# Linear's first three blocks turned by transfers and VectorE from stored rows, the third one's input in the first one's place

## The chip, the cores and the metric

The kernel runs on one core of a Trainium2 chip. The metric is the device time of one execution in microseconds, and the time of the kernel is the median of several runs. A core has TensorE (PE, with its weight loads shown as PEld), VectorE (DVE), ScalarE (ACT), GpSimd (POOL) and SyncE (SP, which here only issues transfers), each with an instruction stream of its own that runs in order.

## What is computed

Two layers over 2 x 1024 tokens of 512 numbers, four sub-layers in all, each followed by a residual sum and a layernorm. The change lies in the second sub-layer, called Linear here, and touches the end of the first one and the start of the third.

```python
x = _layernorm(x + _L0_attn_ref(x, ...))          # state-space layer
x = _layernorm(x + _L0_ffn_ref(x, weight, scale)) # Linear: the place of the change
x = _layernorm(x + _L1_attn_ref(x, ...))          # recurrence: branches, gates, scans
x = _layernorm(x + _L1_ffn_ref(x, ...))           # gated feed-forward

def _L0_ffn_ref(x, weight, scale):                # weight is 512 x 512, of -1, 0 and 1
    out = jnp.einsum('bln,nk->blk', x, weight) * scale
    v_norm = jnp.maximum(jnp.linalg.norm(out, axis=-1, keepdims=True), EPS)
    out = out * (jnp.tanh(v_norm) / (v_norm + EPS))
    o_norm = jnp.maximum(jnp.linalg.norm(out, axis=-1, keepdims=True), EPS)
    return out * jnp.minimum(0.99 / o_norm, 1.0)
```

## The kernel before

The tokens are worked on in four blocks of 512 (`NBLK`), block b in four groups of 128 rows (`NJ`). A block's rows lie in a tile `X[b]` of 128 partitions x 4 x 512. For a product with TensorE the block is needed turned, with its 512 columns on the partitions in four pieces of 128 (`NK`). There are two ways to turn one in this kernel.

`transposed` (L226) does it on TensorE: per piece k four 128x128 transposes (L237) into a PSUM bank, from which ScalarE or VectorE copies. With `split`, ScalarE casts the bank to fp32r (L241), and VectorE subtracts the cast from the bank (L244): two fp32r pieces, `wu0` and `wd0`, stand for one fp32 operand, and each product is made of two matmuls.

The other way has two halves. `load_blocks` (L261) loads the block's rows from DRAM in four DMAs of 256 KB, which set runs of 32 numbers (128 bytes) where the 32x32 squares of the turned block belong. `turn_blocks` (L271) then turns the 32x32 squares within each piece with four VectorE instructions (L273). It needs the rows in DRAM, where `conclude` stores them (`x_mid`, L791, and L799 for block 0).

Linear's block b is the generator `linear(b)` (L968). It makes the two pieces, yields, makes four row groups of products `po` (L987, eight matmuls each) with a scaling on VectorE (L991) and a sum of squares on ScalarE (L993), yielding after two and after four. Then come the chain of small operations for the norms (L997 to L1009), the residual sum (L1011), and `layernorm` with its last step (L291) on POOL, all but one row group of block 0, which is VectorE's. From block 1 on the rows are stored as `x_lin`. Blocks 0, 1 and 2 are turned by `transposed`, the last block by `load_blocks` into `mid` (L1063), `turn_blocks` and `split` (L951), which casts from SBUF (L955) and subtracts (L957).

`conclude` (L762) ends the first layer for a block: per row group j eight matmuls `po` (L770) with a yield in the middle, and VectorE's row sum into `X` (L785). Between the row groups of the last block, `weave` (L304) puts steps of `linear(0)` and `linear(1)`: plan entry i says how many steps follow step i of `conclude`. Then `weave` joins `linear(2)` with the first block's `branches(0)` of the recurrence, which turns X[0] with `transposed` into tile `w4` and makes products with w_x and w_y (`p`, L1069, in `product`). `gates(0)` (L1109) makes products of the convolved `cv`, with `linear(3)` between them.

The program's text sets a priority only: a scheduler orders each engine's instructions, and an instruction under `keep_in_program_order` stays behind everything that stands before it in the text on its engine. Tiles of one tag share a place in a pool, and a pool lays out its tags in the order in which they first appear. The pools `ep` and `wp` lie where the first layer's tiles were; what is loaded there waits for the last reader of what lay there. w_f0 (L900) waits for the scan products' end, X[0] and X[1] (L903) for the last reader of `w_in`, w_x (L909) for POOL's `sums` (L759). Tag `lo` of `ep` is first used by `coming_block` (L962), tag `w4` of `wp` by `branches(0)`; the places of `w0` to `w3` come first. SP issues all these loads from one queue: w_f0, X[0], X[1], the scale row f0s, w_x, w_y, X[2], twelve small parameter loads (`parameters`, L856, whose `softplus` of a_param gives VectorE a dozen small operations), then w_ig, w_ag (L1029) and the first integer weights `st` (L927).

The layers are written out a second time (`later_layers(False)`), behind a test of the weights that is false with these inputs.

Of the kernel before, what the change touches and what calls it, by code (L numbers as in the profile page):

```python
# [9 lines left out]
F32 = mybir.dt.float32  # L10
# [3 lines left out]
ALU = mybir.AluOpType  # L14
PSUM = bass.MemoryType.PSUM

P = 128
TB = 512
NJ = TB // P
D = 512  # L20
NK = D // P
# [16 lines left out]
def model_kernel(ctx: ExitStack, tc: tile.TileContext, t: dict, out: bass.AP):  # L38
    nc = tc.nc
    ctx.enter_context(nc.allow_non_contiguous_dma(reason="small parameter columns"))  # L40
    BATCH, SEQ, _ = t["L0_attn_hidden_states"].shape
    NBLK = BATCH * SEQ // TB
# [3 lines left out]
    x_mid = tc.dram_tile([NBLK, TB, D], F32, name="x_mid")  # L46
# [35 lines left out]
    X = [tokens() for _ in range(3)]  # L82
# [140 lines left out]
        nc.vector.tensor_scalar(r, z, 0.0, None, ALU.max)  # L223
        nc.vector.scalar_tensor_tensor(o, p, 2.0, r, ALU.mult, ALU.add)

    def transposed(pool, b, X, tags=("xT",), split=False, bufs=1, by_act=False, behind=False, soon=False):  # L226


        pieces = [
            pool.tile([P, NK, TB], F32R if split else F32, tag=tag, name=f"{tag}{b}", bufs=bufs)  # L230
            for tag in tags
        ]
        xT = pieces[0]
        for k in range(NK):
            pt = bank("pt")
            for j in range(NJ):
                nc.tensor.transpose(  # L237
                    pt[:, j * P : (j + 1) * P], X[b][:, j, k * P : (k + 1) * P], ident
                )
            if split:  # L240
                copied = nc.scalar.copy(xT[:, k, :], pt)  # L241
                if behind:
                    tc.keep_in_program_order(copied)
                nc.vector.tensor_tensor(  # L244
                    pieces[1][:, k, :], pt, xT[:, k, :].bitcast(F32), ALU.subtract
                )
            elif soon:
                with tc.high_priority():
                    nc.scalar.copy(xT[:, k, :], pt)
            elif k % 2 or by_act:  # L250
                nc.scalar.copy(xT[:, k, :], pt)
            else:
                nc.vector.tensor_copy(xT[:, k, :], pt)
        return pieces
# [6 lines left out]
    def load_blocks(dst, rows, pinned=False):  # L261

        blocks = rows.rearrange("(n t) (k a c) -> a t k n c", t=32, k=NK, c=32)
        for a in range(4):
            load = nc.sync.dma_start(
                dst[32 * a : 32 * a + 32].rearrange("t k (n c) -> t k n c", c=32), blocks[a]
            )
            if pinned:
                tc.keep_in_program_order(load)

    def turn_blocks(dst, src=None, pinned=False):  # L271
        for k in range(NK):
            turned = nc.vector.transpose(dst[:, k, :], (src or dst)[:, k, :])  # L273
            if pinned:
                tc.keep_in_program_order(turned)
# [28 lines left out]
    def weave(main, fill, plan, rest=True):  # L304

        for i, _ in enumerate(main):
            for _ in range(plan[i] if i < len(plan) else 0):
                next(fill, None)
        for _ in fill if rest else ():
            pass  # L310
# [451 lines left out]
    def conclude(b, st):  # L762


        xc, sums = st["xc"], st["sums"]
        rms = sp.tile([P, NJ], F32, tag="rms", name="rms")
        for j in range(NJ):
            po = bank("po")
            for m in range(NX):
                nc.tensor.matmul(  # L770
                    po, xc[:, m, j * P : (j + 1) * P], w_out[:, m, :],
                    start=(m == 0), stop=(m == NX - 1),
                )
                if m == NX // 2 - 1:
                    yield
            if j == 0:
                pss = bank("pss")
                for i in range(NJ):
                    nc.tensor.matmul(
                        pss[:, i : i + 1], sums[:, i * P : (i + 1) * P], ones,  # L780
                        start=True, stop=True,
                    )
                nc.scalar.activation(rms, pss[:, :NJ], AF.Sqrt, bias=eps, scale=1.0 / DI)
                nc.vector.reciprocal(rms, rms)
            nc.vector.scalar_tensor_tensor(  # L785
                X[b][:, j, :], po, rms[:, j : j + 1], X[b][:, j, :], ALU.mult, ALU.add
            )
            yield
        if b:
            layernorm(X[b], pinned=b == NBLK - 1)  # L790
            store_rows(x_mid[b], X[b])  # L791
# [15 lines left out]
    H, before, st = None, None, {}  # L807
# [10 lines left out]
    for b in range(NBLK):  # L818
# [22 lines left out]
        before, st = st, coming  # L841
# [43 lines left out]
    def later_layers(exact, last=None):  # L885
# [4 lines left out]
        X = Y  # L890
# [8 lines left out]
        w_f0 = ep.tile([P, NK, D], F32, tag="wF", name="w_f0" + suffix)  # L899
        nc.sync.dma_start(w_f0, w_f0_source)  # L900
        rows_mid = [x_mid[b].rearrange("(j p) d -> p j d", p=P) for b in range(NBLK)]
        for b in range(2):
            nc.sync.dma_start(X[b], rows_mid[b])  # L903
        w1 = [
            wp.tile([P, NK, D], F32, tag=f"w{i}", name=f"w1{i}{suffix}") for i in range(4)
        ]
# [41 lines left out]
            wf = ep.tile([P, NK, D], F32, tag="wg0", name="wfg")  # L948
            nc.vector.tensor_copy(wf, w_f0)

        def split(x, pieces):  # L951


            for k in range(NK):
                nc.scalar.copy(pieces[0][:, k, :], x[:, k, :])  # L955
                if exact:
                    nc.vector.tensor_tensor(  # L957
                        pieces[1][:, k, :], x[:, k, :], pieces[0][:, k, :].bitcast(F32),
                        ALU.subtract,
                    )  # L960
# [7 lines left out]
        def linear(b):  # L968

            tags = ("wu0", "wd0") if exact else ("wu0",)  # L970
            if b == NBLK - 1:
                turn_blocks(mid)
                w1.append(wp.tile([P, NK, D], F32, tag="w4", name="w14" + suffix))
                xT = [ep.tile([P, NK, TB], WT, tag=tag, name=f"{tag}{b}") for tag in tags]
                split(mid, xT)
                nc.sync.dma_start(w1[4], w_sources["w_out"])
            else:

                xT = transposed(ep, b, X, tags=tags, split=exact, behind=b == 2)
            yield  # L980
            o = ep.tile([P, NJ, D], F32, tag="wF", name="o" + suffix)
            ssq = sp.tile([P, NJ], F32, tag="ssq", name="ssq")
            for j in range(NJ):
                po = bank("po")
                for k in range(NK):
                    for x in xT:
                        nc.tensor.matmul(  # L987
                            po, x[:, k, j * P : (j + 1) * P], wf[:, k, :],
                            start=(k == 0 and x is xT[0]), stop=(k == NK - 1 and x is xT[-1]),
                        )  # L990
                nc.vector.tensor_tensor(o[:, j, :], po, f0s, ALU.mult)  # L991
                junk = ep.tile([P, GW], mybir.dt.bfloat16, tag="junk", name="junk2")
                nc.scalar.activation(junk, o[:, j, :], AF.Square, accum_out=ssq[:, j : j + 1])  # L993
                if j % 2:
                    yield
            norm = sp.tile([P, NJ], F32, tag="norm", name="norm")
            nc.scalar.activation(norm, ssq, AF.Sqrt)  # L997
            v = sp.tile([P, NJ], F32, tag="v", name="v")
            nc.vector.tensor_scalar(v, norm, 1e-7, None, ALU.max)
            f = sp.tile([P, NJ], F32, tag="f", name="f")  # L1000
            nc.scalar.activation(f, v, AF.Tanh)
            nc.vector.tensor_scalar(v, v, 1e-7, None, ALU.add)
            nc.vector.reciprocal(v, v)
            nc.vector.tensor_tensor(f, f, v, ALU.mult)
            nc.vector.tensor_tensor(norm, norm, f, ALU.mult)
            nc.vector.tensor_scalar(norm, norm, 1e-7, None, ALU.max)
            nc.vector.reciprocal(norm, norm)
            nc.vector.tensor_scalar(norm, norm, 0.99, 1.0, ALU.mult, ALU.min)
            nc.vector.tensor_tensor(f, f, norm, ALU.mult)  # L1009
            for j in range(NJ):  # L1010
                nc.vector.scalar_tensor_tensor(  # L1011
                    X[b][:, j, :], o[:, j, :], f[:, j : j + 1], X[b][:, j, :],
                    ALU.mult, ALU.add,
                )
            layernorm(X[b], engine=nc.gpsimd, last=None if b else nc.vector)
            if b:
                store_rows(x_lin[b], X[b])
            yield

        if last:  # L1020
            steps, free = last

            weave(steps, itertools.chain(linear(0), linear(1)), (0, 1, 0, 2, 0, 1, 0, 2, 1))
            free()
        else:
            for _ in itertools.chain(linear(0), linear(1)):
                pass
        for i, name in ((2, "w_ig"), (3, "w_ag")):
            nc.sync.dma_start(w1[i], w_sources[name])  # L1029
# [28 lines left out]
        with tc.tile_pool(name="rec" + suffix, bufs=1, side="right", reuse_waits="tile") as rp:  # L1058
# [125 lines left out]
                yield  # L1184

            st = {}
            weave(branches(0, st), linear(2), (1,) * 4)
            lin = [coming_block(1)]
            bout = row("L1_attn_b_out", D, c1, nc.sync, "scale")
            ys = []  # L1190
# [254 lines left out]
```

## Time and profile before

| what | value |
|---|---|
| median of 3 runs | 1117.68 us (1117.55 to 1117.88) |
| profiled execution | 1116.89 us, span 1115.1 us, mean granted TensorE clock 0.998 |
| TensorE transposes at L237 | 96 in all, 0.273 us each; 64 of them from 416.4 to 458.7 us |
| VectorE transposes at L273 | 40 in all, 0.66 to 0.71 us each |
| `conclude` of the last block | po from 408.8 to 446.3 us |
| `linear(0)`, `(1)`, `(2)`, `(3)` products | from 424.7, 447.8, 461.9 and 500.1 us |
| VectorE busy, 410 to 420, 420 to 430, 430 to 440, 440 to 450 us | 9.26, 3.75, 6.24, 8.87 us |

Times in the text are microseconds from the start of the span. A line such as `416.58 1.81 PE pt L237 x16` in the chain of waits reads: from 416.58 on, for 1.81 us, the chain ran through 16 TensorE instructions of line 237, which write tile `pt`. In a line of the busy times by window stand the window, its length, then busy time and number of instructions for PE, PEld, DVE, ACT and POOL, the granted TensorE clock, the share of the DMA engines that was busy, and GB/s. In a row of one source line stand minimum, median and maximum in ns, then the first and last start in us.

### The profile page before, as it was taken

The page shows a single profiled execution, that of the slowest core. Times are in us where ns is not written, and L with a number is a line of the kernel's source. Part 1 is how long each engine was busy: PE and PEld are TensorE (multiplying, and loading weights), DVE is VectorE, ACT ScalarE, POOL GpSimd, SP SyncE. Part 2 cuts the span into 40 slices and gives each one's busy share as a digit, 9 for nine tenths or more (in the row PEclk, how much of TensorE's full clock was granted, in tenths as well). Part 3 has the DMA queues.
Part 4 walks back from the last instruction along what each step waited for, and adds up shares of the span by engine and source line. Part 5 has one row for each costly group of instructions (what it writes and reads, how often), then busy time and mean ns, then how long its engine had stood idle before and what let it go on. Part 6 is the DMA issues. An engine that isn't in the chain of part 4 may idle for free.

```text
span 1115.1 us, 12073 instructions
## 1 busy us (share of the span) xinstructions
PE 1099.4 (99%) x4450; PEld 663.3 (59%) x4450; DVE 701.4 (63%) x1267; ACT 451.4 (40%) x690; POOL 366.8 (33%) x347
## 2 busy tenths in 40 slices
PE   8999999999999999999999999999999999999996
PEld 5455445445544555745444444447888888888885
DVE  5989797797869676875727437184238866325224
ACT  3334624463454233556653372553223224224223
POOL 1547471565348240254433231236511001001000
PEclk9999999999999999999999999999999999999999
DMA  8005200911210137245650001304544002100001
GB/s 323 21 9 126 91 1 17 253 30 39 105 81 0 39 135 215 57 94 123 113 113 37 1 1 49 27 0 143 189 94 76 1 1 63 14 1 30 8 1 41
DMA packets 122059, 77.04 MB, mean 69 GB/s; under 512 B 94512, under 2 KB 95312, under 8 KB 120456
## 3 DMA queue, kind: packets, MB, share of 16 engines
q1 hardware_dynamic: 120792, 75.77, 25.7%
q8 instruction: 37, 0.61, 0.2%
q10 hardware_dynamic: 976, 0.39, 0.1%
q14 instruction: 30, 0.25, 0.1%
q0 software_dynamic: 224, 0.02, 0.0%
HBM read 59.95 MB, written 16.02 MB: 68 GB/s over the span
## 4 chain that ended last, share of the span: by engine, by line
PE 80%; DVE 11%; ACT 4%; issue 2%; POOL 2%; DMA 1%; SPq 0%; DVEq 0%; ACTq 0%; POOLq 0%
PE pgu L1039 20%; PE p L1069 16%; PE po L1270 10%; PE pg L372 9%; PE px L372 7%; PE po L770 6%; DVE acc L298 3%; PE po L1159 2%; PE py L705 2%; DVE L L578 2%; PE po L987 2%; PE pxt L674 1%; PE pt L237 1%; POOL x L1165 1%; PE py L697 1%
## 5 line engine op out<-in xcount | busy, mean ns | idle before, releaser
L1050 DVE SCALAR_TENSOR_TENSOR h<-pgu,L_ffn_up_scale,sg 128x512 f32<-128x512 f32 x63 | 47.1, 748 | 126.4 <-PE pgu L1039 122.6
L372 PE MATMUL px<-xT,w_in 128*128 128x512 f32 x256 | 114.6, 597 | 0.0
L593 POOL TENSOR_TENSOR L<-L,gm 128x512 f32<-128x512 f32 x64 | 93.5, 1490 | 63.7 <-DVE bdec L588 34.7
L372 PE MATMUL pg<-xT,w_in 128*128 128x512 f32 x256 | 113.5, 594 | 0.0
L770 PE MATMUL po<-w_out,xc 128*128 128x512 f32 x256 | 112.5, 593 | 0.7 <-DVE L L578 0.7
L1069 PE MATMUL p<-cv,w 128*128 128x512 f32 x256 | 110.8, 592 | 0.0
L1039 PE MATMUL pgu<-wF__4239,wg 128*128 128x512 f32 x256 | 101.7, 397 | 0.0
L1039 PE MATMUL pgu<-lo__4240,wg 128*128 128x512 f32 x256 | 100.8, 394 | 0.0
L1039 PE MATMUL pgu<-lo__4240,wu 128*128 128x512 f32 x256 | 100.7, 393 | 0.0
L1039 PE MATMUL pgu<-wF__4239,wu 128*128 128x512 f32 x256 | 100.7, 393 | 0.0
L1270 PE MATMUL po<-wd,hh 128*128 128x512 f32 x252 | 98.3, 396 | 0.3 <-POOL wg L930 0.3
L1270 PE MATMUL po<-wd,hl 128*128 128x512 f32 x252 | 98.3, 396 | 0.2 <-DVE hl L1054 0.2
L1049 ACT ACTIVATE sg<-pgu,L_ffn_gate_scale 128x512 f32<-128x512 f32 x63 | 43.4, 689 | 127.6 <-PE pgu L1039 127.6
L770 PEld LDWEIGHTS po<-w_out,xc 128*128 128x128 f32 x256 | 48.4, 190 | 61.8 <-issue 56.7
L1053 ACT CAST hh<-h 128x512 fp32r<-128x512 f32 x63 | 39.1, 621 | 112.5 <-DVE h L1050 112.3
L1069 PEld LDWEIGHTS p<-cv,w 128*128 128x128 f32 x256 | 48.6, 190 | 60.4 <-issue 58.8
L1069 PE MATMUL p<-xT,w 128*128 128x512 f32 x192 | 82.9, 592 | 0.0
L372 PEld LDWEIGHTS px<-xT,w_in 128*128 128x128 f32 x256 | 47.5, 190 | 57.5 <-issue 55.5
L298 DVE SCALAR_TENSOR_TENSOR acc<-xpad,cols,acc 128x512 f32<-128x512 f32 x72 | 68.5, 953 | 20.0 <-ACT acc L342 15.2
L372 PEld LDWEIGHTS pg<-xT,w_in 128*128 128x128 f32 x256 | 47.3, 190 | 54.2 <-issue 53.1
L1386 POOL TENSOR_TENSOR x<-x,r 128x512 f32<-128x512 f32 x12 | 15.2, 1295 | 195.0 <-DVE r L1385 195.0
L578 DVE TENSOR_TENSOR_SCAN L<-pl,id 128x512 f32<-128x512 f32 x64 | 75.0, 1205 | 4.7 <-ACT pl L572 3.7
(292 smaller groups left out, 1921.9 us busy)
## 6 DMA issues: line engine op xcount, KB each, us to landing
L<-decays SPq DMA_DIRECT2D x12, 1024.0 KB, 8.0
x_mid<-x SPq DMA_DIRECT2D x4, 1024.0 KB, 4.3
x<-x_mid SPq DMA_DIRECT2D x4, 1024.0 KB, 7.5
st<-in_L_ffn_gate_w_dram SPq DMA_DIRECT2D x8, 512.0 KB, 6.4
st<-in_L_ffn_up_w_dram SPq DMA_DIRECT2D x8, 512.0 KB, 4.4
st<-in_L_ffn_down_w_dram SPq DMA_DIRECT2D x8, 512.0 KB, 3.8
x_rec<-x SPq DMA_DIRECT2D x4, 1024.0 KB, 4.3
x<-_attn_hidden_states_dram SPq DMA_DIRECT2D x3, 1024.0 KB, 16.8
```

The source lines that it names most:

```text
L298: tap = nc.vector.scalar_tensor_tensor(acc, xpad[:, k : k + TB], w[:, k : k + 1], acc, ALU.mult, ALU.add)
L372: nc.tensor.matmul(pm[:n, :], w_in[:, k, lo : lo + n], xT[:, k, :], start=(k == 0), stop=(k == NK - 1),)
L578: nc.vector.tensor_tensor_scan(L[:, h, :], pl, id4.rearrange("p j t -> p (j t)"), 0.0, ALU.mult, ALU.add)
L593: nc.gpsimd.tensor_tensor(L[:, h, :], L[:, h, :], st["gm"], ALU.mult)
L705: nc.tensor.matmul(pys[i][hh * HD : (hh + 1) * HD, q, :], dtx[q][:, 2 * i + hh, :], L[:, h, s], start=(first and q == 0), stop=(q == 1), s ...
L770: nc.tensor.matmul(po, xc[:, m, j * P : (j + 1) * P], w_out[:, m, :], start=(m == 0), stop=(m == NX - 1),)
L1039: nc.tensor.matmul(pm, w[g][:, k, cols], x[:, k, :], start=(k == 0 and x is pieces[0]), stop=(k == NK - 1 and x is pieces[-1]),)
L1049: nc.scalar.activation(sg, pgu[0], AF.Silu, scale=gs[:, m : m + 1])
L1050: nc.vector.scalar_tensor_tensor(h, pgu[1], us[:, m : m + 1], sg, ALU.mult, ALU.mult)
L1053: nc.scalar.copy(halves[0], h)
L1069: nc.tensor.matmul(pm, w1[i][:, k, m * P : (m + 1) * P], rhs[:, k, :], start=(k == 0), stop=(k == NK - 1),)
L1270: nc.tensor.matmul(po[j], x[:, j * P : (j + 1) * P], wd[m // GK][:, m % GK, :], start=(m == 0 and x is h[0]), stop=(m == NF - 1 and x is h ...
```

## The change

`linear(b)` no longer uses `transposed`. The stored rows of blocks 0 to 2 are loaded by `load_blocks` (new function `untouched`, four DMAs each): block 0 into tag `lo` behind w_f0, block 1 into tag `w4` behind X[1], and block 2 into `lo` again, once block 0 has been split. `turn_blocks` turns each in place on VectorE, and `split` makes the pieces. The turns of blocks 1 and 2 and the casts of block 2 are kept in program order (block 2's casts were so before), and so are the row sums j = 1 and 2 of the last block's `conclude` and the first small operation (`least`) of block 1's norms. `lo` and `w4` now appear in their pools ahead of the other tags but `wF`. `linear(2)` has one more yield, behind its turn. The steps of the first three blocks are put in an order by hand (`first_two`), and the plans of both `weave` calls are changed.

```diff
-    def transposed(pool, b, X, tags=("xT",), split=False, bufs=1, by_act=False, behind=False, soon=False):
+    def transposed(pool, b, X, tags=("xT",), split=False, bufs=1, by_act=False, soon=False):
...
-                copied = nc.scalar.copy(xT[:, k, :], pt)
-                if behind:
-                    tc.keep_in_program_order(copied)
+                nc.scalar.copy(xT[:, k, :], pt)
...
-            nc.vector.scalar_tensor_tensor(
+            sum_ = nc.vector.scalar_tensor_tensor(
                 X[b][:, j, :], po, rms[:, j : j + 1], X[b][:, j, :], ALU.mult, ALU.add
             )
+            if b == NBLK - 1 and 0 < j < NJ - 1:
+
+                tc.keep_in_program_order(sum_)
             yield
...
         nc.sync.dma_start(w_f0, w_f0_source)
         rows_mid = [x_mid[b].rearrange("(j p) d -> p j d", p=P) for b in range(NBLK)]
+
+        def untouched(b, pool, tag):
+
+            x = pool.tile([P, NK, TB], F32, tag=tag, name=f"raw{b}" + suffix)
+            load_blocks(x, x_mid[b])
+            return x
+
+        raw = [untouched(0, ep, "lo")]
         for b in range(2):
             nc.sync.dma_start(X[b], rows_mid[b])
+        raw.append(untouched(1, wp, "w4"))
...
-        def split(x, pieces):
+        def split(x, pieces, pinned=False):
             for k in range(NK):
-                nc.scalar.copy(pieces[0][:, k, :], x[:, k, :])
+                cast = nc.scalar.copy(pieces[0][:, k, :], x[:, k, :])
+                if pinned:
+                    tc.keep_in_program_order(cast)
...
             tags = ("wu0", "wd0") if exact else ("wu0",)
+            x = mid if b == NBLK - 1 else raw.pop(0)
+            turn_blocks(x, pinned=0 < b < NBLK - 1)
+            if b == 2:
+                yield
             if b == NBLK - 1:
-                turn_blocks(mid)
                 w1.append(wp.tile([P, NK, D], F32, tag="w4", name="w14" + suffix))
-                xT = [ep.tile([P, NK, TB], WT, tag=tag, name=f"{tag}{b}") for tag in tags]
-                split(mid, xT)
+            xT = [ep.tile([P, NK, TB], WT, tag=tag, name=f"{tag}{b}") for tag in tags]
+            split(x, xT, pinned=b == 2)
+            if b == NBLK - 1:
                 nc.sync.dma_start(w1[4], w_sources["w_out"])
-            else:
-
-                xT = transposed(ep, b, X, tags=tags, split=exact, behind=b == 2)
+            elif b == 0:
+                raw.append(untouched(2, ep, "lo"))
             yield
...
-            nc.vector.tensor_scalar(v, norm, 1e-7, None, ALU.max)
+            least = nc.vector.tensor_scalar(v, norm, 1e-7, None, ALU.max)
+            if b == 1:
+
+                tc.keep_in_program_order(least)
...
+        third = linear(2)
+
+        def first_two():
+
+            one, two = linear(0), linear(1)
+            for steps in (one, one, one, two, one, third, two, two, third, two):
+                next(steps)
+                yield
+
         if last:
             steps, free = last
-            weave(steps, itertools.chain(linear(0), linear(1)), (0, 1, 0, 2, 0, 1, 0, 2, 1))
+            weave(steps, first_two(), (0, 1, 0, 3, 0, 1, 0, 2, 1))
             free()
...
-            weave(branches(0, st), linear(2), (1,) * 4)
+            weave(branches(0, st), third, (0, 1, 1, 1))
```

More of the change, by code (lines that the diff above doesn't have):

```diff
@@ L1018, in linear @@
             yield
+        third = linear(2)
[4 more added lines that the diff above has]
+                yield
         if last:
             steps, free = last
-            weave(steps, itertools.chain(linear(0), linear(1)), (0, 1, 0, 2, 0, 1, 0, 2, 1))
+            weave(steps, first_two(), (0, 1, 0, 3, 0, 1, 0, 2, 1))
             free()
         else:
-            for _ in itertools.chain(linear(0), linear(1)):
+            for _ in first_two():
                 pass
```

## The prediction

> **What bounds the kernel now.** I began with the page's first part.
>
> ```profile
> span 1115.1 us, 12073 instructions
> PE 1099.4 (99%) x4450; PEld 663.3 (59%) x4450; DVE 701.4 (63%) x1267; ACT 451.4 (40%) x690; POOL 366.8 (33%) x347
> ```
>
> TensorE is busy for 1099.4 of 1115.1 us, so a matmul that disappears is worth its own length, provided that TensorE finds the next one ready. Next, the chain of waits in the stretch that the change touches (start, length, instruction).
>
> ```profile
> 416.58 1.81 PE pt L237 x16
> 418.38 6.87 PE po L770 x16
> 425.25 7.30 PE po L987 x32
> 432.56 13.73 PE po L770 x32
> 446.29 1.75 PE pt L237 x16
> 448.04 7.47 PE po L987 x32
> 455.51 3.49 PE pt L237 x32
> 459.00 3.44 PE p L1069 x8
> 462.44 3.68 PE po L987 x16
> ```
>
> From 416 to 466 the chain is TensorE alone. L237 is `transposed`: 16 transposes for block 0, 16 for block 1, and 32 for block 2 and `branches(0)` together. The same view further on (its chain followed back from 530 us) leaves TensorE.
>
> ```profile
> 473.97 2.38 issue
> ...
> 478.96 4.13 POOL x L291 x2
> ...
> 489.17 2.74 DVE x L1011 x4
> ...
> 502.39 2.37 PE po L987 x9
> ```
>
> Here POOL's normalization of X[1], then VectorE's end of block 2, decide when `linear(3)` can go on, while TensorE is kept busy with other products: the busy time by windows gives TensorE 10.00 of each 10 us, and 9.86 in 500 to 510. So this second chain has almost no slack, and whatever TensorE gains earlier, it can keep only if this chain moves too.
>
> **Removed.** 48 transposes. By the chain, 1.80 us (416.58 to 418.38), 1.75 (446.29 to 448.04) and half of 3.49: 5.30 us of TensorE. The 12 casts stay on ScalarE, from SBUF at 0.621 us (L955) where they took 0.607 from PSUM (L241), and the 12 subtractions on VectorE at 0.688 (L957) where they took 0.681 (L244): 0.25 us more in all, beside TensorE. 12 PSUM banks are no longer asked for.
>
> **Added on VectorE.** Twelve 128x512 transposes.
>
> ```profile
> L273 DVE STREAM_TRANSPOSE rec<-rec x4: 668/670/705, 719.1 to 720.9; 128x512 f32<-128x512 f32 x4
> ```
>
> At 0.67 us, four take 2.5 us (495.19 to 497.68 in the order of VectorE's work), and three blocks 7.5. What hides them is VectorE's idle time.
>
> ```profile
> 420.00:430.00 10.00, 10.00 (x35) 6.27 (x34) 3.75 (x6) 0.98 (x3) 0.00 (x0) 1.00 0.82 212
> 430.00:440.00 10.00, 10.00 (x30) 5.38 (x29) 6.24 (x30) 7.55 (x13) 0.00 (x0) 1.00 0.78 192
> ```
>
> The third busy figure is VectorE's: 6.25 and 3.76 us are free. Before and after that it is nearly full (9.26 in 410 to 420, 9.72 in 460 to 470).
>
> Block 0: the last weight cast and check on VectorE ends at 418.48 and its X sum at 419.2; 2.5 us of turning gives 421.7, the first subtraction 422.4, the last 424.4. TensorE reaches `linear(0)` 1.8 us earlier than 424.69, at 422.9, and needs its last k after 1.4 us more, at 424.3. Cost 0.1 (0, if the turns slip in among the casts, to 1.5). Block 1: its turn is pinned behind the last scaling (L991) of block 0, so 431.3 to 433.8, with subtractions until about 437; its products come at 444.3. No cost while 7 us of cover last.
>
> **Added on SP's queue.** Twelve DMAs of 256 KB in 128-byte runs. The price is that of `rec`, which ran with no other transfer.
>
> ```profile
> 696.00:698.00 2.00, 2.00 (x6) 0.82 (x5) 0.00 (x0) 0.69 (x1) 0.00 (x0) 1.00 1.45 157
> 698.00:700.00 2.00, 2.00 (x6) 0.89 (x5) 0.00 (x0) 0.00 (x0) 1.26 (x1) 1.00 1.67 130
> ```
>
> The last figure is GB/s: at 130 a block of 1.05 MB takes 8.0 us; the half block of `mid` in 466 to 470 (167, then 95 GB/s) gives 6.4. A row load takes 2.9 (362 GB/s, 436 to 442). SP's own issue of four took 5.6 (`rec`) to 9.8 us (`xT` at 100).
>
> The Trainium skill speaks against this path: "VectorE: DVE Perf Modes", The three transpose paths, and Rules for kernel authors, keeps a 128x128 transpose on TensorE and calls a plain DMA with a transposing access pattern 19 times slower than the hardware's own transposing one. If the row load stood for that fast path, an estimate by the page would be 19 x 2.9 = 55 us a block, and the change would lose tens of us. The trace says 2.2 to 2.8 times a row load; here VectorE turns 32x32 pieces and the DMA only places runs of 32 numbers, so I go by the trace.
>
> Now the queue, in its order.
>
> ```profile
> 415.40 0.37 SPq L909 DMA_DIRECT2D w<-in_L_attn_w_x_dram  x1
> ...
> 427.35 0.51 SPq L93 DMA_DIRECT2D L_attn_a_param<-in_L_attn_a_param_dram  x1
> ```
>
> SP stood 5.0 us before 415.40, for POOL's `sums`. With `w4` first in its pool, raw1 takes the place that w_x had and so this wait. Behind it stand f0s, w_x, w_y, X[2], twelve parameter DMAs, raw2, w_ig, w_ag and `st`. Adding up the DMA time (estimate, from the prices above; the lower end of each with 6.4 us a block): w_f0 to 406; raw0 to 412 to 414; X[0] and X[1] to 418 to 420; raw1 to 425 to 428; f0s (a quarter of a row load) 426 to 429; w_x, w_y, X[2] to 434 to 437; the parameters, 8 us (the slow stretch 426 to 434), to 442 to 445; raw2 to 448 to 453.
>
> What each delay is worth: f0s was issued at 409.92 and is needed by the first L991, now at 425.2. Landing at 429, the four scalings run together and the last still ends at 431.3: nothing. X[0] is no longer turned by TensorE at 416 and is first read at L1011: nothing. w_x is needed at 453 and w_ig at 488: covered by 15 us and more. Two are not covered. The softplus of a_param (L213) sits in VectorE's line; it ran at 431.4, 4 us behind its issue. It would now land at 437 to 440. Its dozen small operations (about 2.3 us) then fall into the chain norm, L1011, layernorm of X[0], POOL L291. That chain ended at 453.8 for transposes at 455.5. Its start moves 1.8 us earlier, and so would its end (452), while the `branches(0)` transposes come at 452 too (455.5 less 1.80 and 1.75). So any delay of VectorE there is paid by TensorE, which has nothing else ready: block 2's pieces need the place of block 1's. From 0, if the softplus waits its turn, to 6.0 if VectorE stands at L213 until 438.5 (X[0] done at 457.7); I take 1.2, about half of the 2.3: that chain is mostly short operations that wait for one another (VectorE is free for 3.76 of 10 us there), and the softplus can fill such gaps.
>
> Block 2: the turn is pinned behind the last row sum (L785), at 444.4, and the split waits for block 1's products to end, at 451.9. Casts 452.5 to 455, subtractions to 456; TensorE is there at 457 (462.4 less 5.3). Cost 0 if raw2 lands by 451, then its lateness. I take 0.
>
> The chain behind 470: block 1's scaling ends 3.6 us earlier, TensorE's arrival at `linear(3)` is 5.3 earlier, less the 1.2 above. It waits 0.5 us today and would wait 0.5 more: (5.3 - 1.2) - 3.6. Bounds 0, with the `cv` products put first, to 4.
>
> **Order and pins.** The pins on two row sums, on `least` and on block 2's casts issue nothing. They put VectorE's row sum j=1 behind block 0's subtractions and j=2 behind block 1's; the banks that these hold are wanted by nobody for 8 us. The first yield of `linear(2)` is only moved. The second copy of the layers is not executed.
>
> **Sum.** 5.30 - 0.1 - 1.2 - 0.5 = 3.5 us of gain. The profiled execution took 1116.89 us (span 1115.1); the median is 0.79 above it. 1116.89 - 3.5 = 1113.4, and on the median's footing 1117.68 - 3.5 = **1114.2 us**. 0.2% is 2.2 us, about what a measurement can tell from no change.
>
> **Rivals.** *All of it is kept* (chance 0.22): gain 4.7, or 5.3 and the 0.5 of today's wait: 1111.9 to 1113.0. For it: VectorE's 10 free us in 420 to 440. Against: X[0]'s chain ends just where it is needed. *Given back to the POOL and VectorE chain* (0.22): TensorE arrives early and stands at X[0] and at `linear(3)`; with X[0] at 457.7 the wait is 5.7 and the time about 1117.68 - 5.3 + 5.7 = 1118.1; between that and half of it, 1115.5 to 1119. For it: the chain shown from 473 to 502. *Slower, by raw2* (0.20): it must wait for block 0's last subtraction (424.4), so that w_ig, w_ag and `st`, which wait for nothing, may be queued first: 3 x 2.9 = 8.7 us on 448 to 453, landing at 457 to 462. VectorE, in order, stands at the pinned turn from 445, and behind it stand block 1's scalings and X[3]'s layernorm; pieces are ready 4 us after landing, at 461 to 466 against 457, and the second chain starts as late. Near 464 that is 7 us, and 2 more for the scalings caught up: 1117.68 - 5.3 + 9 = 1121.4. It decides from a landing after 451, and outweighs the gain from about 457. *The transposes stay*: excluded, the call is gone.
>
> **How the numbers follow.** Forecast (gain 2.3 to 4.7, 1113.0 to 1115.4) 0.36; with the first rival, faster 0.58; same 0.22; slower 0.20. The range runs from 1111.9 to 1120.5, which leaves out about a tenth above, in the last rival; the likeliest case's own range is 1113.0 to 1115.4.
>
> **What would show it.** L237 with 48 instead of 96 matmuls; L273 with 12 more on VectorE at 0.67; `raw` landings at 414, 428, 453 at the latest; a TensorE wait of about 1 us before the transposes at 452, and of 1 us at `linear(3)`. Wrong would be: VectorE standing on a DMA at L213 or at raw2's turn for over 3 us, or a TensorE idle time over 5 us between 420 and 505.

## The result, and the profile after

| kernel | median | profiled execution | span | clock |
|---|---|---|---|---|
| before | 1117.55 us (1116.88 to 1117.88) | 1116.89 us | 1115.1 us | 0.998 |
| after | 1135.72 us (1135.45 to 1136.11) | 1135.45 us | 1133.7 us | 0.988 |

The changed kernel takes 1.0166 times as long (95% interval 1.0153 to 1.0179): 18.2 us more, where 3.5 us less were forecast. The page of the changed kernel, its first part and the row of the granted clock (a digit is tenths of full speed in 1/40 of the span):

```profile
span 1133.7 us, 12010 instructions
...
PE 1100.8 (97%) x4402; PEld 661.8 (58%) x4402; DVE 707.8 (62%) x1279; ACT 449.2 (40%) x688; POOL 366.9 (32%) x347
...
PEclk9999999999999998799999999999999999999998
```
TensorE's busy time grew by 1.4 us although 48 matmuls are gone, and the span grew by 18.6. So TensorE stood still and also ran slower, both in slices 16 and 17 of the clock's row, which are 425 to 482 us.

VectorE's work in that stretch, in its order (start, length, line; in brackets the idle time before it and what ended it). L783 is the row sum, L1006 the scaling, L271 the turn, L969 the subtraction, L1029 the residual sum; raw1 is block 1's loaded tile, f0s the scale row that the scalings read:

```profile
423.91 0.75 DVE L783 SCALAR_TENSOR_TENSOR x<-po,rms,x 128x512 f32<-128x512 f32 x1
444.62 0.75 DVE L783 SCALAR_TENSOR_TENSOR x<-po,rms,x 128x512 f32<-128x512 f32 x1 [19.96 <-PE po L768]
445.29 2.47 DVE L1006 TENSOR_TENSOR o<-po,L_ffn_scale 128x512 f32<-128x512 f32 x4
447.68 2.48 DVE L271 STREAM_TRANSPOSE raw<-raw 128x512 f32<-128x512 f32 x4
450.08 2.46 DVE L969 TENSOR_TENSOR wd<-raw,wu 128x512 fp32r<-128x512 f32 x4
452.45 0.74 DVE L783 SCALAR_TENSOR_TENSOR x<-po,rms,x 128x512 f32<-128x512 f32 x1
...
455.18 2.74 DVE L1029 SCALAR_TENSOR_TENSOR x<-o,f,x 128x512 f32<-128x512 f32 x4
```
In the kernel before, the first scaling, the first residual sum and POOL's normalization of X[0] were:

```profile
427.14 0.69 DVE L991 TENSOR_TENSOR o<-po,L_ffn_scale 128x512 f32<-128x512 f32 x1 [1.10 <-PE po L987]
...
439.11 0.75 DVE L1011 SCALAR_TENSOR_TENSOR x<-o,f,x 128x512 f32<-128x512 f32 x1
...
447.34 6.48 POOL L291 TENSOR_SCALAR x<-x,mv,rs 128x512 f32<-128x512 f32 x3 [31.96 <-PE pt L237]
```
The new order is where most of the loss starts. VectorE ends row sum j=1 at 424.7 and next has the row sum j=3, whose products TensorE ends at 444.6. It stands 19.96 us. The four scalings of block 0 come behind that, though their products are done by 431 and f0s, issued at 424.49, can be there at about 430.5 (where it landed, issued at 424.35, in the kernel with row sum j=3 pinned, below). Then come raw1's turn, its subtractions, row sum j=2, and only then the norms and the residual sum of X[0]: 455.2, where the kernel before had 439.1.

What it does to TensorE is in the chain of waits, further on:

```profile
464.81 2.36 POOL x L289
467.17 4.11 POOL x L289 x2
471.33 3.04 PE pt L237 x13
474.37 4.99 PE p L1096 x8
```
POOL normalizes X[0] from 464.8 (447.3 before), and the transposes of X[0] follow it. TensorE's two long waits, the first for block 1's pieces, the second for X[0]:

```profile
449.55 1.65 PE L1002 MATMUL po<-wfr,wu 128*128 128x512 f32 x3 [4.97 <-ACT wu L965]
...
467.22 0.69 PE L237 MATMUL pt<-ident,x 128*128 128x128 f32 x2 [8.28 <-POOL x L289]
```
Two more waits in the transposes of X[0] took 1.37 and 1.58 us. The eight products that took 3.44 us before took 4.99. The busy times by windows show why (window, length, busy time of PE, PEld, DVE, ACT, POOL, then the granted clock, the busy share of the DMA engines, GB/s):

```profile
445.00:450.00 5.00, 0.45 (x1) 0.45 (x2) 5.00 (x9) 3.91 (x11) 0.00 (x0) 0.67 1.26 137
450.00:455.00 5.00, 5.00 (x16) 3.79 (x16) 4.49 (x15) 2.64 (x6) 0.00 (x0) 0.65 0.82 73
...
465.00:470.00 5.00, 1.16 (x3) 0.47 (x3) 2.47 (x9) 0.41 (x2) 5.00 (x3) 0.50 0.00 0
470.00:475.00 5.00, 3.67 (x14) 3.17 (x15) 0.94 (x3) 2.88 (x8) 1.36 (x3) 0.50 0.00 0
475.00:480.00 5.00, 5.00 (x11) 2.34 (x10) 5.00 (x10) 3.09 (x6) 0.00 (x0) 0.76 0.59 179
```
After each long wait TensorE works on at a lowered granted clock for 4 to 6 us. Busy time times the clock that is missing gives 5.5 us over these windows, 1.9 behind the first wait and 3.6 behind the second and the short ones after it. So: 5.3 us saved, 16.2 us of waits, 5.5 us of slow clock, together 16.4 us lost; VectorE's last instruction of the program stands 17.0 us later (1126.74 against 1109.75). The remaining 1.6 us of the span lie behind the last store: it was issued at 1127.32 and the span ends 6.4 us later, where the kernel before needed 4.8.

### The profile page after: what moved, and what is told of

The parts are those of the page before. It is cut to its first block, busy times and chain, and to the rows that moved or that the text cites. A ratio compares the mean times of both kernels' runs of the same rounds, so it can differ in the third digit from the quotient of the medians.

```text
span 1133.7 us, 12010 instructions
## 1 busy us (share of the span) xinstructions
PE 1100.8 (97%) x4402; PEld 661.8 (58%) x4402; DVE 707.8 (62%) x1279; ACT 449.2 (40%) x688; POOL 366.9 (32%) x347
## 4 chain that ended last, share of the span: by engine, by line
PE 81%; DVE 11%; ACT 3%; POOL 2%; DMA 2%; issue 1%; SPq 0%; DVEq 0%; ACTq 0%; POOLq 0%
PE pgu L1066 20%; PE p L1096 19%; PE po L1297 10%; PE pg L370 9%; PE px L370 7%; PE po L768 5%; PE po L1186 2%; PE py L703 2%; DVE L L576 2%; DVE acc L296 2%; PE po L1002 2%; PE pxt L672 1%; POOL x L1192 1%; DMA cdec<-since 1%; PE py L695 1%
```

## Experiments: what put the row sum first

Theory 1: the planner that orders each engine counts f0s as late, because a block load now stands ahead of it in SP's queue, and so plans row sums ahead of the scalings that need f0s. Theory 2: the pins (`keep_in_program_order`) on the row sums make the order. Theory 3: transfers (raw2 above all) are late in fact. Theory 4: VectorE's added turns fill it.

**f0s ahead of raw1.** One line of the changed kernel moved:

```diff
+        f0s = par["f0s"] = row("L0_ffn_scale", D, c1, nc.sync, "scale")
         raw.append(untouched(1, wp, "w4"))
...
-        f0s = par["f0s"] = row("L0_ffn_scale", D, c1, nc.sync, "scale")
```

> The changed kernel with one line moved: the load of the FFN's scale row (f0s) is queued ahead of raw1's load instead of behind it. Theory 1 (the planner counts f0s as late because a block load stands ahead of it, and so puts the row sum j=3 ahead of block 0's four scalings, where VectorE stood 19.96 us): the scalings run before 433 us, X[0] is normalized before 452, the 8.28 us of TensorE before the transposes of X[0] vanish; raw1's turn may still stand behind the row sum at 444.6, which leaves some 5 us before block 1's products and the slow ones behind them. 1116 to 1121 us. Theory 2 (the pins on the row sums make the order): the order stays, 1133 to 1137. Theory 3 (what is late is data, raw2's above all, in the queue): the queue carries the same bytes, 1132 to 1137. Theory 4 (VectorE's added transposes fill it): they are all still there, over 1130.

Measured: 1123.66 us, 1.0063 times before (1.0048 to 1.0078). VectorE's order in this kernel:

```profile
431.03 0.69 DVE L1006 TENSOR_TENSOR o<-po,L_ffn_scale 128x512 f32<-128x512 f32 x1 [0.90 <-PE po L1002]
...
444.76 0.75 DVE L783 SCALAR_TENSOR_TENSOR x<-po,rms,x 128x512 f32<-128x512 f32 x1 [2.21 <-PE po L768]
445.43 2.48 DVE L271 STREAM_TRANSPOSE raw<-raw 128x512 f32<-128x512 f32 x4
```
The last scaling ends at 431.7 instead of 447.8, and TensorE no longer waits for X[0]. Some 11 to 12 us come back from moving one 256 KB load by one place. But row sum j=3 still stands ahead of raw1's turn, so block 1's pieces are late (2.15 us of TensorE), and block 2's as well (4.37 us before 465.19). The time was 2.7 us above the expected range.

**Row sum j=3 pinned too**, transfers as in the changed kernel:

```diff
-            if b == NBLK - 1 and 0 < j < NJ - 1:
+            if b == NBLK - 1 and j:
```

> The changed kernel with the last row sum (j=3) pinned in program order as well; every transfer stays where it is. Theory 1 (an order that was planned on a late f0s): the scalings now stand ahead of j=3 and wait for f0s itself, which lands at about 429: they end by 432, raw1's turn by 435, block 1's products find their pieces, and both idle times of TensorE (4.97 and 8.28 us) go. 1113 to 1119 us. Theory 2 (pins are what delays): one more pin makes it no better, 1135 or more. Theory 3 (late transfers): nothing is moved in the queues, so 1132 to 1137. Theory 4 (added VectorE work): over 1130.

Measured: 1123.93 us, 1.0062 times before (1.0047 to 1.0078). VectorE's rows, then POOL's normalization of X[0] and the first of TensorE's transposes of X[0]:

```profile
430.57 2.48 DVE L1006 TENSOR_TENSOR o<-po,L_ffn_scale 128x512 f32<-128x512 f32 x4 [5.90 <-DMA L_ffn_scale<-in_L_ffn_scale_dram]
432.97 2.48 DVE L271 STREAM_TRANSPOSE raw<-raw 128x512 f32<-128x512 f32 x4
435.37 2.46 DVE L969 TENSOR_TENSOR wd<-raw,wu 128x512 fp32r<-128x512 f32 x4
...
440.49 2.74 DVE L1029 SCALAR_TENSOR_TENSOR x<-o,f,x 128x512 f32<-128x512 f32 x4
...
451.87 6.48 POOL L289 TENSOR_SCALAR x<-x,mv,rs 128x512 f32<-128x512 f32 x3 [36.49 <-DVE sp L222]
454.28 0.69 PE L237 MATMUL pt<-ident,x 128*128 128x128 f32 x2 [2.39 <-POOL x L289]
```
Now the scalings stand ahead of j=3 and wait for what they really need: f0s, which lands at 430.5. With the same transfers in the same order, 11 to 12 us come back: theories 3 and 4 cannot be the bulk. What is left is a wait for X[0] (2.39 and, between its parts, 1.37 and 1.58 us) and the slow clock behind it; 5 us more than expected.

**The kernel before, with one load added**, read by nothing:

```diff
+        if exact:
+            idle = wp.tile([P, NK, TB], F32, tag="w4", name="idle")
+            load_blocks(idle, x_mid[1])
         f0s = par["f0s"] = row("L0_ffn_scale", D, c1, nc.sync, "scale")
```

> The kernel before, with one thing added: a load of x_mid[1] in turned blocks (1.05 MB, into the place w4, read by nothing) ahead of f0s. No transpose by VectorE, no pin, all 96 transposes on TensorE. Theory 1: the plan again puts row sums ahead of block 0's scalings; VectorE stands at one of them until about 439, the normalization of X[0] ends some 8 to 10 us later than 453.8 and TensorE waits for it before the transposes of X[0]: 1124 to 1131 us. Theories 2 and 4 (pins, added VectorE work): neither is there, so 1117 to 1119. Theory 3 (transfers late in fact): 8 us more in the queue, f0s lands about 425 and is needed at 425; parameters 8 us later, up to 1121.

Measured: 1130.44 us, 1.0121 times before (1.0106 to 1.0137). The row sum and the scalings (L994 here) on VectorE, X[0] on POOL, TensorE's wait:

```profile
439.45 0.75 DVE L785 SCALAR_TENSOR_TENSOR x<-po,rms,x 128x512 f32<-128x512 f32 x1 [13.43 <-PE po L770]
440.12 2.47 DVE L994 TENSOR_TENSOR o<-po,L_ffn_scale 128x512 f32<-128x512 f32 x4
...
460.38 6.48 POOL L291 TENSOR_SCALAR x<-x,mv,rs 128x512 f32<-128x512 f32 x3 [45.03 <-DVE sp L218]
462.78 0.69 PE L237 MATMUL pt<-ident,x 128*128 128x128 f32 x2 [7.17 <-POOL x L291]
```
VectorE stands 13.43 us at a row sum, the scalings run at 440.1 instead of from 427.1, X[0] is 13.0 us later, and TensorE waits 7.17 us and more. None of the change's turns, pins and saved transposes is in this kernel: a block load ahead of f0s is enough for most of the loss.

**No pins on the row sums:**

```diff
-            if b == NBLK - 1 and 0 < j < NJ - 1:
+            if False:
```

> The changed kernel with the pins on the row sums j=1 and j=2 left out, all transfers as they are. Theory 1 (f0s planned late makes the order): the row sums still go ahead of block 0's scalings, so VectorE still stands at one until 444: 1130 to 1138 us. Theory 2 (the pins made the order): the scalings come first again, 1113 to 1122.

Measured: 1139.62 us, from one execution, 1.6 us above the expected range. VectorE:

```profile
442.11 0.75 DVE L783 SCALAR_TENSOR_TENSOR x<-po,rms,x 128x512 f32<-128x512 f32 x1 [12.26 <-PE po L768]
448.97 0.75 DVE L783 SCALAR_TENSOR_TENSOR x<-po,rms,x 128x512 f32<-128x512 f32 x1 [6.12 <-PE po L768]
449.64 2.47 DVE L1006 TENSOR_TENSOR o<-po,L_ffn_scale 128x512 f32<-128x512 f32 x4
```
Both free row sums, j=2 (12.26 us of waiting in front of 442.11) and j=3, go ahead of the scalings. The pins of the change are not the cause. They held j=1 and j=2 back and left j=3 free.

Together these show, for 11 to 12 of the 18 us, that the place of f0s behind a block load makes the order, and that the order costs the time. That the planner counts f0s as late is theory 1's reading of it: what it reckoned for the load is not in any trace.

## Experiments: what is left when the order is mended

Theory A: between block 0's last scaling (431) and the end of the first layer's products (445) VectorE has room for the norms and the statistics of X[0], or for block 1's turn and subtractions (4.9 us), not for both in time. Rival B: the added loads delay the queue. Rival C: any turn on VectorE costs more than it saves.

**f0s and both block loads first**, all row sums pinned (the places of `w0` to `w3` are allocated ahead of raw1's):

```diff
+        f0s = par["f0s"] = row("L0_ffn_scale", D, c1, nc.sync, "scale")
         raw = [untouched(0, ep, "lo")]
+        raw.append(untouched(1, wp, "w4"))
         for b in range(2):
             nc.sync.dma_start(X[b], rows_mid[b])
-        raw.append(untouched(1, wp, "w4"))
```

> The changed kernel with f0s, raw0 and raw1 queued right behind w_f0 and ahead of X[0] and X[1], the four weight places allocated ahead of them (so that raw1 waits for nothing), and all row sums pinned. Theory 1: scalings of block 0 end by 429, raw1's turn by 434, X[0] normalized by 450, no idle time of TensorE over 1 us between 420 and 470: it keeps most of the 5.3 us of the transposes taken out, 1112 to 1115.5 us, faster than both. Theory 2 (pins): slower than before, over 1120. Theory 3 (late data: X[0], X[1] are now behind two block loads, raw2 is no earlier): 1118 or more. Theory 4 (added VectorE work): over 1125.

Measured: 1125.22 us, 1.0075 times before (1.0061 to 1.0088). Theory 1 missed it by 10 us, and taken alone the run lies in the ranges of theories 2 to 4. The trace says where: the scalings were in time (the last one from 430.91) and raw1 had landed, but raw1's turn took VectorE from 435.81, so that the residual sum of X[0] came at 441.26 and its normalization on POOL at 451.96, and TensorE waited 2.19, 1.37 and 1.58 us for it. So theory 4 had a point, for one turn out of three. That gave theory A.

**Block 0 alone by transfers**, f0s and then raw0 queued behind w_f0, the rest as before:

```diff
+            elif b in (0,):
+                x = raw.pop(0)
+                turn_blocks(x)
+                xT = [ep.tile([P, NK, TB], WT, tag=tag, name=f"{tag}{b}") for tag in tags]
+                split(x, xT)
             else:
                 xT = transposed(ep, b, X, tags=tags, split=exact, behind=b == 2)
...
+            if b == NBLK - 1 and j == 1:
+                tc.keep_in_program_order(sum_)
```

> The kernel before with block 0 alone turned by transfers and VectorE: raw0 is loaded behind w_f0 and f0s, the turn stands ahead of the row sum j=1 (pinned), blocks 1 and 2 stay on TensorE. Theory A (after the order is mended, what is left of the loss is VectorE's time between block 0's last scaling and the end of the last block's po, about 431 to 445 us: the normalization of X[0] fits there, block 1's turn and subtractions of 4.9 us beside it do not): block 0's turn lies ahead of that stretch, so its 1.8 us are kept: 1114.5 to 1116.5 us. Rival B (the added block loads delay the queue: parameters, softplus, X[1]): one block load of 8 us is ahead of all of these, 1118 to 1121. Rival C (any turn on VectorE costs more than it saves): 1118 or more.

Measured: 1115.92 us, 0.9986 times before (0.9977 to 0.9995). The residual sum (L1028 here) and POOL's normalization of X[0]:

```profile
435.85 2.74 DVE L1028 SCALAR_TENSOR_TENSOR x<-o,f,x 128x512 f32<-128x512 f32 x4
...
444.41 6.49 POOL L291 TENSOR_SCALAR x<-x,mv,rs 128x512 f32<-128x512 f32 x3 [28.99 <-DVE spos L872]
```
X[0]'s chain starts 3.3 us earlier than before (435.85 against 439.11), no wait of TensorE is listed between 420 and 510 us, and the last store is issued 1.70 us earlier: block 0's 1.80 us of transposes are kept.

**Block 1 alone by transfers**: the changed kernel with blocks 0 and 2 on TensorE again and all row sums pinned, f0s still behind raw1:

```diff
+            if b in (0, 2):
+                xT = transposed(ep, b, X, tags=tags, split=exact)
+            else:
+                x = mid if b == NBLK - 1 else raw.pop(0)
+                turn_blocks(x, pinned=b == 1)
```

> The changed kernel with blocks 0 and 2 turned by TensorE again and all row sums pinned: block 1 alone by transfers and VectorE. Theory A: its turn and subtractions (4.9 us) stand between block 0's scalings and its chain of norms, X[0] is normalized 3 to 5 us later than in the kernel before (453.8), TensorE waits for it and then runs at a lower granted clock: 1119 to 1125 us, though the transfers are a third of the change's. Rival B (the queue): one block load, as with block 0 alone, within 1 us of that one's time. Rival C (any turn costs alike): the same as block 0 alone.

Measured: 1125.94 us, 1.0076 times before (1.0061 to 1.0092), 1 us above the expected range. The turn, the subtractions, the residual sum, block 1's first scaling, the reciprocal of X[0]'s layernorm, POOL, TensorE:

```profile
433.13 2.48 DVE L271 STREAM_TRANSPOSE raw<-raw 128x512 f32<-128x512 f32 x4
435.53 2.45 DVE L969 TENSOR_TENSOR wd<-raw,wu 128x512 fp32r<-128x512 f32 x4
...
442.12 2.74 DVE L1029 SCALAR_TENSOR_TENSOR x<-o,f,x 128x512 f32<-128x512 f32 x4
...
449.25 0.69 DVE L1006 TENSOR_TENSOR o<-po,L_ffn_scale 128x512 f32<-128x512 f32 x1 [1.24 <-PE po L1002]
...
454.90 0.17 DVE L287 RECIPROCAL rs<-rs 128x4 f32<-128x4 f32 x1
...
455.24 6.47 POOL L289 TENSOR_SCALAR x<-x,mv,rs 128x512 f32<-128x512 f32 x3 [39.95 <-DVE sp L222]
457.65 0.69 PE L237 MATMUL pt<-ident,x 128*128 128x128 f32 x2 [4.14 <-POOL x L289]
```
The same four turns and four DMAs as with block 0, 10 us dearer: rivals B and C fall. The place of f0s is not it either: block 0's scalings ran from 427.06 to 433.2, as before. The 4.9 us stand in front of the norms, and the residual sum comes 3.0 us later than before (442.12 against 439.11). X[0] begins on POOL 7.9 us later, so 4.9 us more are lost behind the residual sum. There VectorE's order has block 1's scalings, each waiting for its products, ahead of the last aggregate of X[0]'s statistics (449.93) and of the reciprocal: again ready work behind waiting work. With both block loads first it was the same (scaling at 447.63, last aggregate at 448.24) although the softplus of a_param came only at 462.43, so the softplus is not the main cause. TensorE waits 7.09 us and then runs at 0.50 to 0.88. Saved 1.75, waited 7.1, slow clock 2.7 us (windows 455 to 470): 8.0 us, which is how much later the last store is issued.

**Blocks 0 and 2 by transfers**, block 1 by TensorE, f0s first:

```diff
+        f0s = par["f0s"] = row("L0_ffn_scale", D, c1, nc.sync, "scale")
         raw = [untouched(0, ep, "lo")]
...
-        raw.append(untouched(1, wp, "w4"))
...
+            if b == 1:
+                xT = transposed(ep, b, X, tags=tags, split=exact)
```

> The changed kernel with block 1 turned by TensorE again, and f0s ahead of raw0: blocks 0 and 2 by transfers and VectorE. Theory A: both turns lie outside the stretch of 431 to 445 us; TensorE has 3.5 us less to do, and reaches X[0] 1.8 us earlier, as X[0] itself; block 2's turn stands behind the layernorm of X[3], with its pieces about when TensorE comes. 1113 to 1116 us. Rival B (the queue's delay): raw2 and raw0 are 16 us of transfers, 1119 to 1124. Rival C: over 1120.

Measured: 1117.02 us, 0.9995 times before (0.9986 to 1.0004): no difference, 1 us above the expected range. X[0] was in time (POOL from 446.62), but block 2's pieces came 1.02 us late at 460.43; `linear(3)` began at 500.17, where it began at 498.51 with block 0 alone and at 500.09 before (POOL's normalization of X[1] began at 477.51, with block 0 alone at 471.41), and the last store went out 0.2 us later than before. With block 2 by transfers nothing of its own transposes is kept, and what block 0 alone brought is gone too. Block 1's place in the order also differs between the two kernels, so the 1.1 us between them are not shown to be block 2's alone.

**A written-out order.** raw1 turned early, directly behind block 0's subtractions; the scalings pinned; raw1's casts and subtractions behind X[0]'s chain. Blocks 0 and 1 by transfers, block 2 by TensorE:

```diff
+            for steps in (one, two, one, one, one, one, two, two, two, two):
...
+                scaled = nc.vector.tensor_tensor(o[:, j, :], po, f0s, ALU.mult)
+                if b < 2:
+                    tc.keep_in_program_order(scaled)
...
+            if b == 0:
+                yield
             layernorm(X[b], engine=nc.gpsimd, last=None if b else nc.vector)
```

> Blocks 0 and 1 by transfers and VectorE, block 2 by TensorE, with the order on VectorE written out: f0s, raw0 and raw1 are loaded ahead of X[0], raw1 is turned right behind block 0's subtractions (about 424.4 to 427, where VectorE has idle time), then block 0's scalings, its norms, residual sum and statistics of X[0], and only then raw1's casts and subtractions (to about 445.5). Theory A (what was lost behind the mended order is VectorE's time between 431 and 445 us): nothing of the turn lies there now, X[0] is normalized by 452 and TensorE is there at 452, so both blocks' 3.5 us are kept but for what the second chain takes: 1113.5 to 1116 us. Rival D (turns and 128-byte transfers cost in themselves, wherever they stand, by slowing other work): the same work as with block 1 alone plus block 0's, 1120 or more. Rival E (only block 0's turn is free, since a_param's softplus comes late): X[0]'s chain is held up by L213, 1117 to 1121.

Measured: 1115.15 us, 0.9982 times before (0.9973 to 0.9991), the lowest median of the study, though its interval overlaps that of block 0 alone. raw1's turn, the residual sum, POOL, then raw1's subtractions:

```profile
426.71 2.49 DVE L273 STREAM_TRANSPOSE raw<-raw 128x512 f32<-128x512 f32 x4 [0.69 <-DMA raw<-x_mid]
...
437.83 2.74 DVE L1035 SCALAR_TENSOR_TENSOR x<-o,f,x 128x512 f32<-128x512 f32 x4
...
444.67 7.52 POOL L291 TENSOR_SCALAR x<-x,mv,rs 128x512 f32<-128x512 f32 x3 [27.28 <-DVE rs L289]
444.99 2.30 DVE L971 TENSOR_TENSOR wd<-raw,wu 128x512 fp32r<-128x512 f32 x3
```
Two blocks are turned by VectorE, and from 420 to 470 us TensorE waits once, 0.42 us. This profiled execution took 1116.60 us: in it `linear(0)` began at 425.00, 2.0 us later than with block 0 alone, from a wait of 2.20 us before 128.54 (0.24 us there with block 0 alone), far ahead of the change. Reckoned from there X[0] begins on POOL 1.7 us earlier than with block 0 alone. Rivals D and E fall.

**The same with all three blocks:**

```diff
+            for steps in (one, two, one, one, one, one, two, two, two, third, third, two):
```

> The same written-out order with all three blocks by transfers and VectorE (raw2 in raw0's place, its turn behind block 1's scalings, its subtractions behind the layernorm of X[3]). Theory A: blocks 0 and 1 keep their 3.5 us; block 2's pieces come near 462, 3 to 4 us behind TensorE, which then also runs at a lower clock: 1115 to 1120 us. If block 2's pieces are in time: 1112 to 1114. Rival D (cost of the turns and transfers themselves): 1122 or more.

Measured: 1121.03 us, 1.0040 times before (1.0027 to 1.0054), 1 us above the expected range. Block 2's turn, TensorE's wait, block 2's subtractions:

```profile
455.02 2.49 DVE L271 STREAM_TRANSPOSE raw<-raw 128x512 f32<-128x512 f32 x4 [1.87 <-DMA raw<-x_mid]
...
461.58 0.73 PE L1002 MATMUL po<-wfr,wu 128*128 128x512 f32 x2 [3.97 <-ACT wu L965]
...
463.10 2.49 DVE L969 TENSOR_TENSOR wd<-raw,wu 128x512 fp32r<-128x512 f32 x4
```
raw2 lands at 455.0, 2.6 us after block 1's products have ended (452.4), and its subtractions come after the layernorm of X[3]; TensorE waits 3.97 us and is granted 0.78 and 0.88 in the next two windows of 5 us. The third block is what turns a gain of 2.4 us into a loss of 3.5; of these 5.9 us, 1.8 lie behind the issue of the last store (6.6 us to the end of the span against 4.8).

## Why the prediction was wrong

- **The step that failed** is block 1's: "its turn is pinned behind the last scaling (L991) of block 0, so 431.3 to 433.8 ... No cost while 7 us of cover last". It took VectorE's order from the trace of before and asked only what each pin holds back. The scaling itself was nowhere held in place: row sum j=3, not pinned, went ahead of it, the turn ran at 447.7, and TensorE waited 4.97 us for block 1's pieces. A pin keeps its own instruction behind what is written before it; it keeps no other instruction from going ahead.
- **f0s.** "Landing at 429, the four scalings run together ... nothing" costed the transfer and left out the order that its new place brings about. With the order mended it cost little, as foreseen (430.5, one wait of 5.90 us on a VectorE with nothing else to do); in the order as planned it cost 11 to 12 of 18 us.
- **X[0]'s chain** was named as uncovered and mis-sized: 1.2 us, and up to 6.0 from the softplus. With the order mended it costs 5.3 us of waits and 3.4 of slow clock (row sum j=3 pinned too, windows 450 to 465). The softplus is the small part, under 1 us (its operations between 443.15 and 451.73 move their neighbours by 0.05 to 0.13 us each). The larger part had no term in the sum: block 1's turn and subtractions, put at no cost, stand in front of the norms (residual sum at 440.49, with block 0 alone at 435.85), and behind it block 1's scalings stand ahead of X[0]'s reciprocal (11.4 us from the residual sum to POOL, with block 0 alone 8.6).
- **The granted clock** had no term in the sum. Behind each wait of 4 us or more, short waits after it counted in, it cost 1.9 to 3.6 us more: these two in the changed kernel, 2.1 to 2.7 with the unread load, with f0s ahead and with block 1 alone.
- **Removed and added work** was right: 48 matmuls fewer, twelve turns more, four in 2.48 us. Block 0 was right to 0.1 us: TensorE at `linear(0)` at 422.98 (422.9 foretold), and kept by itself it brings 1.6 us. With both block loads first they moved at 139 to 147 GB/s from 408 to 420 us, 7.1 to 7.5 us each, within the 6.4 to 8.0 of the estimate. The 55 us that the factor of the Trainium skill's "VectorE: DVE Perf Modes" would have made did not show.
- **The rivals.** The slower one had the sign and not the mechanism: in the changed kernel raw2 was queued ahead of w_ig and nobody stood at it. Its mechanism does show where the rest is mended, with raw2 at 455.0 in the last kernel. "Given back to the POOL and VectorE chain" is what remains with the order mended, at 7 us instead of 0.4 over before.
- "A TensorE idle time over 5 us between 420 and 505" was named as a sign of being wrong, and it came at 467.2.

## What to carry to other kernels

When a scheduler orders the engines, moving a load moves the order too: look at who reads it, and whether something that is not tied down can be planned ahead of that reader and then wait long on the chip. Price a moved step in the stretch in which it will run: the same four turns brought 1.6 us in one place and cost 8.4 in another, where a chain of short operations stood behind them and, once late, fell behind other work that was itself waiting. And where TensorE is the bound, add the slow clock behind a long wait: here 1.9 to 3.6 us for each wait of 4 us or more.

## What was not expected of the hardware

- **The granted clock after waits.** Waits of 1.02 and 2.15 us left the windows of 5 us that hold them at 1.00; after 4.14, 4.37, 7.17 and 8.28 us it fell to about 0.50. Three short ones of 2.39, 1.37 and 1.58 us with three transposes between them did the same (0.50 in 455 to 460, with all row sums pinned). The Trainium skill, "TensorE: Matmul & The Clock Gate", Part 1, gives a window of about 3.4 us of idleness after which the clock is halved, and about as long of work to bring it back; the single waits here lie on both sides of that and agree. The clock was back at 1.00 in the changed kernel after some 4 us of work (449.6 to 453.5) and some 6 (471.3 to 477.4), so no sooner than that.
- **The end of the span.** In the six kernels that load all three blocks (the changed one and five of the experiments) the span ends 6.3 to 6.6 us behind the issue of the last store, in the five experiments with fewer block loads and in the kernel before 4.8 to 4.9 (profiled executions). Why some 1.6 us are lost there was not found out.
